# Layer 3's sums in a four-layer graph kernel: which density groups stand between the last tiles, and where the ninth tile is loaded

## The chip, the cores and the metric

The kernel runs on one core of one Trainium2 chip. The metric is the device time of one execution in microseconds. Three runs of the kernel before gave 861.08, 863.25 and 863.85 us, a median of 863.25 us. One further execution was profiled; all views below are of that one.

## The reference

Four graph layers follow one another on x (2708 nodes, 128 features) and a dense 0/1 adjacency matrix of 2708 x 2708. The change touches the fourth, called layer 3:

```python
def _L3_gnn_ref(X, A, W, a):
    XW = jnp.matmul(X, W)
    s_col = jnp.matmul(XW, a[0, :f])
    s_row = jnp.matmul(XW, a[0, f:])
    Z1 = jax.nn.leaky_relu(s_row[:, None] + s_col[None, :], negative_slope=0.01)
    den = jnp.exp(Z1)
    num = jnp.matmul(A, den)
    att = jnp.where(num != 0, den / jnp.where(num != 0, num, 1.0), 0.0)
    H = jnp.matmul(A, jnp.matmul(att, XW))
    return H
...
h = jnp.maximum(_layernorm(x, axis=-1), 0.0)
x = x + _L3_gnn_ref(h, adj, L3_gnn_W, L3_gnn_a)
```

`den[i, j]` depends only on the sum of a row score and a column score. Where that sum is positive, `den` is a product of two exponentials, and where it is negative, a product of two others. So with the nodes sorted by score, a whole chunk of nodes can be summed at once, and only the nodes near the place where the sign changes need their own values.

## The kernel before

The nodes lie in T = 22 tiles of 128, the last with 20 rows. In the general stage `rest(exact, ...)`, of which the exact variant runs with this adjacency, layer 3 goes through these steps.

1. *Ranks and chunks.* Each node's rank by score is counted, and the nodes are cut into 22 chunks (`ge`, `lt`, `wts`).
2. *Sums.* `sums(t)` (line 818) loads the 128 rows of tile t of the transposed adjacency with a DMA on the SP queue (line 826, 1354 KB by the profile's count) and multiplies them on TensorE (line 833) with two sets of chunk weights. A tile is 18 matmuls: three banks, three bf16 pieces of the weights, two halves. All 22 tiles accumulate into the same three PSUM banks, `acc` 0 to 2. Where the rows go depends on t:
   - tiles 0 to 3 (`t < NEARLY`, which is 4) go into `early_rows`: two parts of dflat, then hn, then yT;
   - three later tiles (`LATER`) go into `regained`, which are hT, row_b, hs and yT, by number: tile 8 into hs, tile 19 into hT, tile 20 into row_b;
   - all others go through the ring `steps`, tag `rows`, which has four buffers. A tile's load waits until the sums of the tile four places earlier in the ring are done.
3. *Places.* Meanwhile VectorE works out which nodes belong to which chunk, with small products on TensorE (`placed`, line 862). Its last results are the operands `c_two` and `r_hi` of the densities.
4. *Densities.* There are NS = 44 half steps, taken in eleven groups of four. `densities(s0)` (line 1080) makes a diagonal operand on VectorE (line 1084), multiplies it with ones on TensorE into a bank of the two-bank pool `ps` (line 1091), evacuates the four quarters of the bank in turn on VectorE (line 1099) and ScalarE (line 1097), and finishes with one VectorE instruction (line 1100) and one exponential on ScalarE (line 1101). The result lies in `dmat`, which is dflat.
5. *Evacuation and return.* The three banks of sums go to hn (lines 1117 and 1118), are cut into a high and a low part in yT (lines 658 and 1121), and are written to DRAM as `pre_d` by two DMAs on the SP queue and two on the ScalarE queue (line 1124). This block has raised priority.
6. *Attention loop.* For each half step the adjacency rows of 128 listed nodes are gathered into one of the four `regained` buffers (`gather_rows`, line 660), a few rows of `pre_d` are gathered over them (`carry`, line 1128), and the buffer is cast into a `rows` tile (line 1163). Both gathers are indirect DMAs issued by GpSimd (line 647). Then come products with the densities (line 1201), a logarithm (line 1206), an exponential (line 1215) and a second product (line 1145). This loop has 22 steps.

The order of instructions on each engine is fixed when the program is built. A planner takes the instruction that is earliest in the program among those that it holds ready at an estimated time; raised priority goes ahead. Instructions given to `tc.keep_in_program_order` keep their order among themselves on their engine. In the kernel before, the seven calls of `densities` up to `FIRST = 28` stand in the program ahead of `sums(4)` to `sums(21)`, the three gathers into hT, row_b and hs come after the sums, and the other four groups follow. Neither the sums nor the density products are marked, so the planner places them freely on TensorE. The products of the loop at line 1201 and 1145 are marked, and so are the row gathers and the casts.

Of the kernel before, what the change touches and what calls it, by code (L numbers as in the profile page):

```python
# [19 lines left out]
def kernel(  # L20
# [19 lines left out]
    nc = tc.nc  # L40
# [3 lines left out]
    T = -(-N // P)  # L44
# [17 lines left out]
    def rows(t):  # L62
        return min(P, N - t * P)
# [16 lines left out]
    def cols(t):  # L80
        return slice(t * P, (t + 1) * P)
# [11 lines left out]
    def bank():  # L93
        return ps.tile([P, 512], F32, tag="bank", name="bank")
# [70 lines left out]
    NS = 2 * NE  # L165
# [108 lines left out]
    with ExitStack() as stack:  # L274
# [3 lines left out]
        def load_rows(src, t):  # L278
            return fill(stream.tile([P, N], F32, tag="a", name="a"), src, t)
# [67 lines left out]
        for t in range(T):  # L347
            a = first_rows[t] if t < 3 else load_rows(adj, t)
# [119 lines left out]
    for i, at in enumerate(SUMS):  # L468
        m = (is_lo, is_hi)[i % 2]
# [16 lines left out]
    def rest(exact, stack3):  # L486
# [173 lines left out]
        def gather_rows(a, s):  # L660

            m = gather(a, adj_t[:, :], row_i[:, s : s + 1])
            tc.keep_in_program_order(m)
            return a
# [4 lines left out]
        with tc.tile_pool(name="tab", bufs=1) as tab, tc.tile_pool(name="tabs", bufs=2) as tabs:  # L669
# [17 lines left out]
            for b in range(NB):  # L687
# [26 lines left out]
                for c in range(new.start, new.stop, 3):  # L714
                    m = min(3, new.stop - c)
# [13 lines left out]
            for c in range(0, T, 3):  # L729
                m = min(3, T - c)  # L730
# [8 lines left out]
                for q in range(m):  # L739
                    t = c + q  # L740
# [77 lines left out]
            def sums(t):  # L818
                r = rows(t)
                if t < NEARLY:  # L820
                    a = early_rows[t]
                elif t in LATER:
                    a = regained[LATER[t]]
                else:
                    a = steps.tile([P, N], F32, tag="rows", name="rows")
                nc.sync.dma_start(a[:r, :], adj_t[t * P : t * P + r, :])
                if exact:
                    a = a.bitcast(BF16).rearrange("p (n h) -> p n h", h=2)[:, :, 1]
                for b in range(3):
                    for i, w in enumerate(wts):  # L830
                        for h in range(2):
                            lo, hi = BLK[b + 3 * h]
                            nc.tensor.matmul(  # L833
                                accs[b][64 * h : 64 * h + 2 * NC, : hi - lo],
                                w[:r, t, :],
                                a[:r, lo:hi],
                                start=(t == 0 and i == 0),
                                stop=(t == T - 1 and i == len(wts) - 1),
                            )

            early_rows = [dflat[:, :N], dflat[:, N : 2 * N], hn.rearrange("p t d -> p (t d)")[:, :N], yT[:, :N]]
            NEARLY = len(early_rows)

            LATER = {NEARLY + 4: 2, T - 3: 0, T - 2: 1}


            ohc = tt("ohc", [P, T, NC], ge[:, :, :NC], ge[:, :, 1:], ALU.subtract)
# [32 lines left out]
            for t in range(NEARLY):  # L880
                sums(t)
# [193 lines left out]
            r_hi = row("r_hi", NS)  # L1075
            nc.vector.tensor_scalar(r_hi, r_step, slope_hi, None, ALU.mult)

            FIRST = 28

            def densities(s0):  # L1080
                n = min(4, NS - s0)
                diag = tabs.tile([P, 4, P], F32, tag="diag", name="diag")
                z = dmat[:, s0 : s0 + n, :]
                nc.vector.tensor_tensor(
                    diag[:, :n],
                    ident[:, None, :].to_broadcast([P, n, P]),
                    c_two[:, s0 : s0 + n, None].to_broadcast([P, n, P]),
                    ALU.mult,
                )
                p = bank()  # L1090
                nc.tensor.matmul(  # L1091
                    p[:, : n * P], ones, diag[:, :n].rearrange("p s q -> p (s q)"), start=True, stop=True
                )
                for q in range(n):
                    by = r_hi[:, s0 + q : s0 + q + 1]
                    if q % 2:
                        nc.scalar.activation(z[:, q, :], p[:, cols(q)], AF.Identity, bias=by, scale=slope_hi)
                    else:
                        nc.vector.tensor_scalar(z[:, q, :], p[:, cols(q)], slope_hi, by, ALU.mult, ALU.add)
                nc.vector.scalar_tensor_tensor(z, z, flatter, z, ALU.mult, ALU.max)  # L1100
                nc.scalar.activation(z, z, AF.Exp)

            for s0 in range(0, FIRST, 4):
                densities(s0)
            for t in range(NEARLY, T):
                sums(t)
            for q in range(3):
                gather_rows(regained[q], q)
            for s0 in range(FIRST, NS, 4):
                densities(s0)  # L1110
            flat = hn.rearrange("p t d -> p (t d)")
            pre_hi = yT[:, :HALF]
# [35 lines left out]
        with tc.tile_pool(name="att", bufs=2) as attp:  # L1148
# [29 lines left out]
            for s in range(NE):  # L1178
# [19 lines left out]
                for b, (lo, hi) in enumerate(E0):  # L1198
                    num = bank()
                    for i, (d, a) in enumerate(products):  # L1200
                        m = nc.tensor.matmul(  # L1201
                            num[:, : hi - lo], d, a[:, lo:hi], start=(i == 0), stop=(i == len(products) - 1)
                        )
# [81 lines left out]
    with tc.If(some_low > 0) as general:  # L1285
        with ExitStack() as s3:
            rest(False, s3)
    with general.Else():
        with ExitStack() as s3:
            rest(True, s3)  # L1290
# [32 lines left out]
```

## Time and profile before

| what | us |
|---|---|
| median of three runs | 863.25 |
| profiled execution, whole | 860.91 |
| its span, first to last instruction | 859.1 |
| mean granted TensorE clock | 0.935 of full |
| first sums on TensorE start | 445.91 |
| last sums start (18 instructions, 2.00 us) | 520.30 |
| pre_d write leaves the queue, takes 7.80 | 527.59 |
| first product of the attention loop | 541.31 |
| first instruction of the last product's chain | 786.67 |

Times in the table are counted from the start of the span. Over the whole span TensorE's matmuls are busy for 727.6 us (85%), VectorE 583.0 us (68%), ScalarE 535.8 us (62%) and GpSimd 193.5 us (23%). These shares are means over stages with different limits, so they say little of one stage. For a change in one stage the chain of waits and the timeline there are read instead.

The SP queue, which issues the loads of the sums, looks like this between 404 and 502 us. The columns are the start, the time from the first to the last issue of the group, the engine, the line, the operation, what is written from what, and the count:

```profile
404.47 0.33 SPq L826 DMA_DIRECT2D hn<-in_adj_t_dram  x1
416.34 0.33 SPq L826 DMA_DIRECT2D hs<-in_adj_t_dram  x1
462.69 28.40 SPq L826 DMA_DIRECT2D rows<-in_adj_t_dram  x10
491.18 0.44 SPq L826 DMA_DIRECT2D hT<-in_adj_t_dram  x1
491.72 0.46 SPq L826 DMA_DIRECT2D row_b<-in_adj_t_dram  x1
501.57 0.30 SPq L826 DMA_DIRECT2D rows<-in_adj_t_dram  x1
```

The load into hn is tile 2, the one into hs is tile 8, the ten into `rows` are tiles 9 to 18, and the last four lines end with tile 19, tile 20 and the short tile 21.

### The profile page before, as it was taken

The page shows a single profiled execution, that of the slowest core. Times are in us where ns is not written, and L with a number is a line of the kernel's source. Part 1 is how long each engine was busy: PE and PEld are TensorE (multiplying, and loading weights), DVE is VectorE, ACT ScalarE, POOL GpSimd, SP SyncE. Part 2 cuts the span into 40 slices and gives each one's busy share as a digit, 9 for nine tenths or more (in the row PEclk, how much of TensorE's full clock was granted, in tenths as well). Part 3 has the DMA queues.
Part 4 walks back from the last instruction along what each step waited for, and adds up shares of the span by engine and source line. Part 5 has one row for each costly group of instructions (what it writes and reads, how often), then busy time and mean ns, then how long its engine had stood idle before and what let it go on. Part 6 is the DMA issues. An engine that isn't in the chain of part 4 may idle for free.

```text
span 859.1 us, 9007 instructions
## 1 busy us (share of the span) xinstructions
PE 727.6 (85%) x3113; PEld 436.7 (51%) x3113; DVE 583.0 (68%) x1112; ACT 535.8 (62%) x595; POOL 193.5 (23%) x161
## 2 busy tenths in 40 slices
PE   3599999995996979978659592699999999989996
PEld 2333333332775857755226331455555555555785
DVE  5499879786834263357988984566776667655854
ACT  3889999995845474446850052678777777767000
POOL 3000000012201010002000101656666666620010
PEclk9889999997897989988879997799999999999999
DMA  9034444724997989966404956677777777785993
GB/s 336 3 136 189 167 165 186 304 76 153 355 402 275 358 341 394 409 269 234 157 1 160 403 237 238 231 290 265 272 285 273 263 286 271 283 302 231 424 427 128
DMA packets 39476, 218.63 MB, mean 254 GB/s; under 512 B 5108, under 2 KB 13999, under 8 KB 25359
## 3 DMA queue, kind: packets, MB, share of 16 engines
q1 hardware_dynamic: 27704, 150.19, 45.1%
q0 software_dynamic: 8624, 65.76, 20.9%
q10 hardware_dynamic: 3090, 1.99, 0.7%
q8 instruction: 27, 0.44, 0.2%
q14 instruction: 31, 0.25, 0.1%
HBM read 214.12 MB, written 3.79 MB: 254 GB/s over the span
## 4 chain that ended last, share of the span: by engine, by line
PE 12%; DMA 10%; DVE 10%; POOL 7%; issue 7%; ACT 6%; POOLq 0%; DVEq 0%; ACTq 0%
DMA hs<-in_adj_t_dram 4%; DMA yT<-pre_d,pre_i 4%; PE acc L1145 3%; PE bank L1201 3%; PE acc L833 2%; ACT rows L1163 2%; POOL hT L647 2%; PE acc L224 2%; POOL hs L647 2%; POOL yT L647 1%; PE bank L1091 1%; POOL xw L647 1%; ACT row_a L747 1%; ACT e L1215 1%; DVE bits L744 1%
## 5 line engine op out<-in xcount | busy, mean ns | idle before, releaser
L1201 PE MATMUL bank<-rows,d_hi 128*128 128x512 f32 (+1 forms) x264 | 106.6, 408 | 37.7 <-DVE d_hi L1170 19.0
L224 PE MATMUL acc<-rows,h_hi 128*128 128x512 f32 (+1 forms) x264 | 107.1, 410 | 9.4 <-ACT rows L529 5.6
L1145 PE MATMUL acc<-e,xw 128*128 128x512 f32 (+1 forms) x264 | 104.3, 545 | 0.0
L1206 ACT ACTIVATE ln<-bank,tiny 128x512 f32<-128x512 f32 x132 | 79.6, 632 | 32.2 <-PE bank L1201 32.2
L224 PE MATMUL acc<-rows,h_lo 128*128 128x512 f32 (+1 forms) x264 | 98.6, 390 | 0.2 <-DVE h_lo L506 0.2
L1201 PE MATMUL bank<-rows,d_lo 128*128 128x512 f32 (+1 forms) x264 | 98.5, 385 | 0.0
L1201 PEld LDWEIGHTS bank<-rows,d_hi 128*128 128x128 f32 x264 | 51.2, 194 | 66.7 <-ACT ln L1206 29.1
L1209 DVE TENSOR_TENSOR e<-e,ln 128x1536 f32<-128x1536 f32 (+2 forms) x66 | 69.6, 1094 | 18.2 <-ACT ln L1206 17.9
L358 DVE SCALAR_TENSOR_TENSOR tau<-tau,e_hi,a 128x1536 f32<-128x1536 f32 (+1 forms) x44 | 70.5, 1623 | 10.2 <-DMA a<-in_adj_dram 5.5
L1145 PEld LDWEIGHTS acc<-e,xw 128*128 128x128 f32 x264 | 48.4, 190 | 52.6 <-issue 52.6
L355 ACT ACTIVATE tau<-row_a,e_neg,e_lo 128x1536 f32<-128x1536 f32 (+1 forms) x44 | 65.7, 1503 | 3.9 <-PE bank L367 3.7
L224 PEld LDWEIGHTS acc<-rows,h_hi 128*128 128x128 f32 x264 | 52.6, 200 | 24.0 <-ACT rows L529 8.5
L224 PEld LDWEIGHTS acc<-rows,h_lo 128*128 128x128 f32 x264 | 52.7, 200 | 12.2 <-issue 2.2
L367 PE MATMUL bank<-tau,ones_at 128*32 128x512 f32 (+1 forms) x264 | 51.8, 566 | 8.3 <-DVE tau L358 8.3
L224 PE MATMUL acc<-yT,hs 128*128 128x512 f32 x132 | 56.7, 567 | 0.0
L1215 ACT ACTIVATE e<-e 128x2708 f32<-128x2708 f32 x22 | 54.2, 2462 | 3.2 <-DVE e L1209 3.2
L224 PE MATMUL acc<-row_b,hs 128*128 128x512 f32 x132 | 55.3, 557 | 0.0
L1201 PEld LDWEIGHTS bank<-rows,d_lo 128*128 128x128 f32 x264 | 51.5, 195 | 7.1
L224 PE MATMUL acc<-rows,y_hi 128*128 128x512 f32 x132 | 49.2, 379 | 4.8 <-DVE rows L1278 2.9
L224 PE MATMUL acc<-rows,y_lo 128*128 128x512 f32 x132 | 47.7, 376 | 0.0
L529 ACT CAST rows<-dflat 128x1536 fp32r<-128x1536 f32 (+1 forms) x26 | 34.2, 1330 | 20.7 <-DMA dflat<-in_adj_dram 11.6
L173 POOL TENSOR_TENSOR rstd<-isq,neg_half 128x4 f32<-128x4 f32 (+1 forms) x24 | 23.5, 982 | 99.8 <-DVE isq L172 85.0
(411 smaller groups left out, 1394.8 us busy)
## 6 DMA issues: line engine op xcount, KB each, us to landing
a<-in_adj_dram SPq DMA_DIRECT2D x21, 1354.0 KB
rows<-in_adj_t_dram SPq DMA_DIRECT2D x17, 1354.0 KB
dflat<-in_adj_t_dram SPq DMA_DIRECT2D x9, 768.0 KB
rows<-in_adj_t_dram SPq DMA_DIRECT2D x9, 768.0 KB
dflat<-in_adj_dram SPq DMA_DIRECT2D x9, 768.0 KB
rows<-in_adj_dram SPq DMA_DIRECT2D x9, 768.0 KB
dflat<-in_adj_t_dram SPq DMA_DIRECT2D x5, 1354.0 KB
hs<-in_adj_t_dram SPq DMA_DIRECT2D x5, 1354.0 KB
```

The lines of the kernel that those rows point to most:

```text
L173: nc.gpsimd.tensor_tensor(dst, s[:, :n], neg_half[:, :n], ALU.pow)
L224: nc.tensor.matmul(accs[b][:, : hi - lo], w, moving[:, lo - at : hi - at], start=start and i == 0, stop=stop and i == len(parts) - 1,)
L355: nc.scalar.activation(tau[:, :w], row_a[:, h0:h1], AF.Relu, bias=e_neg[:, t : t + 1], scale=e_lo[:, t : t + 1])
L358: nc.vector.scalar_tensor_tensor(tau[:, :w], tau[:, :w], e_hi[:, t : t + 1], a[:, h0:h1], ALU.add, ALU.mult)
L367: nc.tensor.matmul(den[g : g + 32, : hi - lo], ones_at[:, b // GR, :], tau[:, lo - h0 : hi - h0], start=(t == 0 and b < GR), stop=(t == T ...
L529: m = nc.vector.tensor_copy(r, a) if i % 2 and i > 4 else nc.scalar.copy(r, a)
L647: return nc.gpsimd.indirect_dma_start(out=out, out_offset=None, in_=src, in_offset=bass.IndirectOffsetOnAxis(ap=idx, axis=0),)
L1145: m = nc.tensor.matmul(accs[b][:, : hi - lo], xw, e[:, lo:hi], start=(s == 0), stop=(s == NE - 1))
L1201: m = nc.tensor.matmul(num[:, : hi - lo], d, a[:, lo:hi], start=(i == 0), stop=(i == len(products) - 1))
L1206: nc.scalar.activation(ln[:, lo:hi], num[:, : hi - lo], AF.Ln, bias=tiny)
L1209: tc.keep_in_program_order(nc.vector.tensor_sub(e[:, beg:hi], e[:, beg:hi], ln[:, beg:hi]))
L1215: tc.keep_in_program_order(nc.scalar.activation(e, e, AF.Exp))
```

## The change

It has four parts.

1. Tile 8 is loaded into `early_rows[2]`, the hn buffer that tile 2 had. Tile 9 takes hs. The ring `rows` then holds 14 tiles of the sums in place of 15.
2. The matmuls of the sums from tile 8 on are marked to keep their program order.
3. The matmul of each density group is marked in the same way.
4. `FIRST` is 3 and counts groups. In the program no group stands ahead of the sums; one group follows each of `sums(17)`, `sums(18)` and `sums(19)`. The other eight groups follow the three gathers.

```diff
                 if t < NEARLY:
                     a = early_rows[t]
+                elif t == NEARLY + 4:
+                    a = early_rows[2]
                 elif t in LATER:
                     a = regained[LATER[t]]
...
-                            nc.tensor.matmul(
+                            m = nc.tensor.matmul(
                                 accs[b][64 * h : 64 * h + 2 * NC, : hi - lo],
...
+                            if t >= NEARLY + 4:
+                                tc.keep_in_program_order(m)
...
-            LATER = {NEARLY + 4: 2, T - 3: 0, T - 2: 1}
+            LATER = {NEARLY + 5: 2, T - 3: 0, T - 2: 1}
...
-            FIRST = 28
+            FIRST = 3
...
                 p = bank()
-                nc.tensor.matmul(
+                m = nc.tensor.matmul(
                     p[:, : n * P], ones, diag[:, :n].rearrange("p s q -> p (s q)"), start=True, stop=True
                 )
+                tc.keep_in_program_order(m)
...
-            for s0 in range(0, FIRST, 4):
-                densities(s0)
             for t in range(NEARLY, T):
                 sums(t)
+                if T - 2 - FIRST <= t < T - 2:
+                    densities(4 * (t - T + 2 + FIRST))
             for q in range(3):
                 gather_rows(regained[q], q)
-            for s0 in range(FIRST, NS, 4):
+            for s0 in range(4 * FIRST, NS, 4):
                 densities(s0)
```

## Prediction

> **What bounds the kernel now.** I read the page's slices first, then the chain of waits around layer 3's sums, then each engine's timeline there, then windows. The slices show where to look: TensorE's busy row falls to 1 in one slice of the last third, at about 525 to 540 us.
>
> ```profile
> PE   3599999995996979978659592699999999989996
> DMA  9034444724997989966404956677777777785993
> ```
>
> The chain, from the last sums to the first step of the attention loop (columns: start, us, what):
>
> ```profile
> 508.82 1.05 PE bank L1091 x2
> 509.88 2.13 PE acc L833 x18
> 512.01 1.92 PE bank L1091 x4
> 513.92 1.93 PE acc L833 x18
> 515.85 1.07 PE bank L1091 x2
> ...
> 526.87 0.62 DVE yT L1121
> ...
> 527.59 7.80 DMA pre_d<-yT
> ...
> 536.39 3.04 DMA hT<-pre_d,pre_i
> ...
> 539.45 1.59 DVE rows L1163
> ```
>
> L833 is the sums, L1091 the density products. They alternate on one chain, so each density group ahead of the last sum delays everything below: evacuating the sums, writing them to pre_d, gathering them back, the loop. TensorE's timeline gives the ends (the bracket is idle time before):
>
> ```profile
> 485.03 5.53 PE L833 MATMUL acc<-rows,wts 128*44 128x450 bf16 x39
> 494.59 3.68 PE L1091 MATMUL bank<-diag,ones 128*128 128x512 f32 x4 [4.03 <-DVE diag L1084]
> ...
> 520.30 2.00 PE L833 MATMUL acc<-rows,wts 20*44 20x452 bf16 x18
> 541.31 0.77 PE L1201 MATMUL bank<-rows,d_hi 128*128 128x512 f32 x1 [19.01 <-DVE d_hi L1170]
> ```
>
> The sums end at E = 522.3 (520.30 + 2.00). TensorE has stood 4.03 us for the first density operand, and then 19.01 us for the gathered sums. Windows tell whether the sums could have been earlier (columns: window, length, then busy us of PE, PEld, DVE, ACT and POOL, clock, DMA share, GB/s):
>
> ```profile
> 484.60:499.40 14.80, 10.77 (x59) 4.30 (x57) 12.66 (x31) 1.59 (x4) 4.07 (x4) 0.77 0.98 391
> 499.40:506.20 6.80, 6.80 (x38) 2.41 (x37) 5.69 (x12) 4.22 (x9) 0.00 (x0) 1.00 0.99 401
> 506.20:518.60 12.40, 11.98 (x66) 4.40 (x64) 10.65 (x23) 7.60 (x17) 0.94 (x1) 1.00 0.09 18
> ```
>
> Until 506.2 the adjacency rows stream at 390 to 400 GB/s; then DMA is idle (share 0.09) for 12 us with TensorE full. So up to 506 the rows are the bound, and from there TensorE, by the density products. Adding up the bytes of the sync queue's packets, in tiles of 1.387 MB, gives the landings: tile 9 at 468.0, 12 at 478.0, 15 at 488.3, 16 at 492.2, 17 at 495.9, 18 at 499.4, 19 at 502.7, 20 (with the short tile 21) at 506.1: 3.47 us each on average.
>
> **What the Trainium skill says.** (1) "PSUM — Partial Sum Buffer", Engine vs sequencer instructions: matmuls start and complete in program order, and the ScalarE and VectorE queues are strict FIFO. The trace agrees: by the landings tile 15 was there at 488.3, but its sums stood behind the density product that waited to 494.59. (2) The same page, PSUM bank collisions: two engines must not touch one bank and quadrant together, ScalarE beside VectorE included. So the four quarters of a density bank go one after another; the trace shows 0.41 us on VectorE and 0.46 us on ScalarE in turn. (3) "DMA: Bandwidth & Descriptors", Issuing engines are not separate DMA queues: all share 16 engines. The pre_d write (4 x 232.7 KB) took 7.80 us with three row gathers of 1.387 MB in flight. (4) "TensorE: Matmul & The Clock Gate", Part 1: idle TensorE drops to half clock. The four L1091 after the 4.03 us idle took 3.68 us, where later pairs take 1.05.
>
> **The change part by part.**
>
> *Eight of eleven density groups leave the stretch of the sums.* A group costs TensorE one pair, 1.05 us. Removed from TensorE before E: 8 x 1.05 = 8.4 us, and the 4.03 us wait with its slow first products (3.68 - 2.10 = 1.6 us), since tiles 15 to 17 now come ahead of the first density product. Without the rows' bound that is 14.0 us, E = 508.3.
>
> *The three groups that stay.* The fixed order is tile 17, group 0, tile 18, group 1, tile 19, group 2, tile 20, tile 21. A tile's 18 sums take 1.93 us, a group 1.05: 2.98 together, less than the 3.47 us between landings, so the rows hide them. Group 0's operand is ready at 494.55 as before (VectorE's chain to L1084 isn't touched). Sums of tile 17 end about 495.4, so the new fixed wait holds nobody; behind it stand tile 18 and all later sums, which have not landed.
>
> *The ninth tile.* Tile 8 goes to hn, free when tile 2's sums end (453.9), in place of hs, which it had from 416.34; hs takes tile 9, and the ring of four holds 14 tiles in place of 15. Before, the sync queue stood from 416.74 to 462.69 for the first ring slot, with DMA idle. Now tile 9 can load at 416 and tile 8 at 454 in that idle time; tile 8 is needed at 467.7 and takes some 2 + 3.3 us, so it is there at about 459.3. This costs nothing (if SP has it behind the ring's load instead, it lands near 468, some 0.5 us late). After 462.7 one tile less is to load: tile 20 lands one tile earlier, about 502.8. Against that: a ring slot opens only when its sums are done, and TensorE stands at L862 to 483.42 for VectorE. If L862 keeps its place inside tile 12's sums, tile 16's load starts 2.5 us late. The planner may place L862 a tile later, which costs nothing. I take half, so 504.1; ends 502.8 and 505.3.
>
> *The new end.* Sums started 1.3 us after the landing (tile 11: 474.76 to 476.06). E = 504.1 + 1.3 + 2 x 1.93 = 509.3, gain 13.0; 508.0 to 511.3 if the landing is 502.8 to 506.1.
>
> *After E.* The three gathers on the POOL queue follow the sums of tiles 19 and 20 and the free hs: about E - 5.4, E - 1.5, E - 0.2, where before they went at E - 5.65, E - 1.15 and E + 0.46. So pre_d meets the same traffic, and its 7.80 us stays. Evacuation (522.21 to 527.5) has raised priority and stays E + 5.2. The gathered sums are cast (L1163) at E + 17.15.
>
> *Where the eight groups go.* Their products need 8.4 us of an idle TensorE. Their elementwise half is dearer: without TensorE in the way the period was 1.8 us a group:
>
> ```profile
> 517.30 0.75 DVE L1100 SCALAR_TENSOR_TENSOR dflat<-dflat,flatter 128x512 f32<-128x512 f32 x1
> ...
> 519.10 0.75 DVE L1100 SCALAR_TENSOR_TENSOR dflat<-dflat,flatter 128x512 f32<-128x512 f32 x1 [0.20 <-ACT dflat L1097]
> ...
> 520.89 0.75 DVE L1100 SCALAR_TENSOR_TENSOR dflat<-dflat,flatter 128x512 f32<-128x512 f32 x1 [0.72 <-ACT dflat L1097]
> ```
>
> 8 x 1.8 = 14.4 us from E + 5.2 is E + 19.6, about E + 19 with what fits into the evacuation's gaps. The cover ends at E + 17.15; past it the casts for the loop queue behind on VectorE. I charge 2.0 us; ends 0 (the casts go ahead, and only TensorE's first products are late) and 7 (2.36 us a group, the period while TensorE was shared: 5.2 + 18.9 - 17.15). TensorE may enter the loop warmer: its first 9 products took 0.63 us, later ones 0.39, at most 9 x 0.24 = 2.2 us; taken as nothing, because the chain at the loop's start runs through gathers and casts.
>
> *Sum.* 13.0 - 2.0 = 11.0 us. The loop (541 to 787) and the last product start from this point and shift whole. On the profiled execution (860.91 us, span 859.1) that is 849.9. It lies 2.3 us under the median of 863.25, and the same 11.0 us against the median gives 852.2: **852**.
>
> **Rivals.** *A, the cover is full:* casts are not delayed, and the rows come at the early end: 522.3 - 508.0 = 14.3 us, 849. For it: later groups are first needed several loop steps on. Against: a FIFO VectorE with 14.4 us of work in a 12 us gap.
>
> *B, a small gain:* ring slots open late (landing 506.1, E = 511.3, gain 11.0), and the groups run at 2.1 us, halfway between the two periods, so 16.8 + 5.2 - 17.15 = 4.9 us late: gain 6.1, 857. For it: 9.3 us of waiting for sums on the sync queue before the last row load. Against: that load was 0.2 MB and late for nobody.
>
> *C, slower:* the evacuation's copies get queued behind the density groups on VectorE and ScalarE; one in-order queue then holds back pre_d. Price: 1.8 to 2.36 us for each group ahead, against 13.0 of gain; it decides from 5.5 to 7.2 groups on. All eight at 2.36 us: 18.9 - 13.0 = 5.9 us slower, 869; at 1.8, 1.4 slower. For it: the queues are fixed when the kernel is built, on estimated times. Against: the copies carry raised priority, and the groups' products stand behind the last sums on TensorE, so they can't be ready sooner.
>
> *D, it cancels:* C's mechanism with about seven groups, 863; or the fixed order changes little, since the planner had already put the sums where they now are. Against the latter: seven groups before E in the chain above and in TensorE's timeline.
>
> **How the numbers follow.** Forecast 0.58 (848 to 856), A 0.12, B 0.15, C 0.11, D 0.04. 846.5 to 859 takes in the forecast, A and B and leaves out C, D and a little: about 0.17. A measurement here tells 0.3%, 2.6 us, from no change. Faster 0.58 + 0.12 + 0.15 = 0.85; same 0.04; slower 0.11.
>
> **What would show it.** Right: TensorE's timeline has tiles 15 to 17 ahead of the first L1091, just three pairs before the last sums, these ending near 509, and eight pairs in the former 19 us idle; DMA waits return before the sums of tiles 18 to 20; the first L1201 comes near 530. Wrong: sums still ending past 515; evacuation copies starting later than 1 us after E; the cast L1163 more than 4 us behind its gather; or a loop longer than 245 us, which gives the gain back. A tile 8 waited for near 468 would show the buffer swap as a cost.

## The result, and the profile after

The changed kernel takes 852.05 us (median of four runs, 850.04 to 853.49) against 863.15 us before (four runs, 861.08 to 863.85): a ratio of 0.9874 with a 95% interval from 0.9847 to 0.9900. A second set, six runs against sixteen, gave 853.77 and 863.58 us, ratio 0.9880 (0.9850 to 0.9911). The forecast was 852.

The slices of the page show the hole filled: the digit 1 in TensorE's row has gone.

```profile
PE   3599999995996979978649785798999989989997
```

TensorE's timeline of the changed kernel, from the first sums (L835 is the sums, L1095 the density products, L1206 the loop's first product, L1150 its second; the bracket is idle time before):

```profile
444.04 0.95 PE L835 MATMUL acc<-dflat,wts 128*44 128x452 bf16 x4 [5.04 <-DVE wts L813]
...
483.19 7.30 PE L835 MATMUL acc<-rows,wts 128*44 128x450 bf16 x57
493.00 3.45 PE L835 MATMUL acc<-rows,wts 128*44 128x452 bf16 x18 [2.51 <-DMA rows<-in_adj_t_dram]
496.39 1.12 PE L1095 MATMUL bank<-diag,ones 128*128 128x512 f32 x2
...
499.37 1.12 PE L1095 MATMUL bank<-diag,ones 128*128 128x512 f32 x2
...
502.35 1.13 PE L1095 MATMUL bank<-diag,ones 128*128 128x512 f32 x2
...
505.53 2.00 PE L835 MATMUL acc<-rows,wts 20*44 20x452 bf16 x18
507.46 1.98 PE L1095 MATMUL bank<-diag,ones 128*128 128x512 f32 x4
513.57 4.25 PE L1095 MATMUL bank<-diag,ones 128*128 128x512 f32 x4 [4.12 <-DVE diag L1088]
...
533.44 0.76 PE L1206 MATMUL bank<-rows,d_hi 128*128 128x512 f32 x1 [4.70 <-DVE d_hi L1175]
...
550.88 4.75 PE L1150 MATMUL acc<-e,xw 128*128 128x512 f32 x12
```

Three groups stand between the last sums, TensorE waits for a row load (2.51 us) instead of a density operand, and the sums end at 507.5. The chain of waits now has the load of tile 20 in it, where it had sums and density products in turn:

```profile
488.25 15.31 DMA row_b<-in_adj_t_dram
...
503.60 3.12 PE acc L835 x27
```

The chain gives this stretch to the load, but only just: from 493.00 to the end of the sums TensorE has no wait longer than 0.12 us, because the sums of tile 17 took 3.45 us behind their wait (granted clock 0.53) where a tile takes 2.00 elsewhere. In a second profile of the changed kernel they took 2.00, and TensorE waited 0.82, 0.18 and 0.79 us for tiles 18, 19 and 20; there the rows hide the three groups.

The windows agree (window, length, busy us of PE, PEld, DVE, ACT and POOL, clock, DMA share, GB/s). The rows run out in the window from 499.40 (share 0.50), and the window that had DMA idle at share 0.09 now has the gathers in it:

```profile
499.40:506.20 6.80, 6.67 (x50) 2.94 (x50) 4.95 (x9) 3.11 (x7) 0.94 (x1) 1.00 0.50 162
506.20:518.60 12.40, 7.48 (x23) 2.32 (x19) 10.21 (x22) 5.75 (x13) 1.88 (x2) 0.78 0.92 368
```

What came before the first sums differed by 1.9 us between the two first profiles, with the same work in it, so distances are counted from the first sums. With a second profile of each kernel, in us:

| distance | before | before again | changed | changed again |
|---|---|---|---|---|
| first sums to end of last sums (E) | 76.4 | 77.6 | 63.5 | 63.2 |
| E to the loop's first product | 19.0 | 19.0 | 25.9 | 25.8 |
| first sums to the loop's first second product | 114.0 | 116.1 | 106.8 | 106.1 |
| the loop, first product to last second product | 245.1 | 246.5 | 245.3 | 243.7 |
| span | 859.1 | 860.0 | 851.7 | 850.7 |

The means give 13.6 us gained at E, 6.8 at the loop's first product, 8.6 at its first second product and 8.4 in the span. The timed runs say 10 to 11. The distances inside the loop differ by 1 to 2 us between two profiles of one kernel, so small differences there say little.

### The profile page after: what moved, and what is told of

It is laid out like the page before. It is cut to its first block, busy times and chain, and to the rows that moved or that the text cites. A ratio compares the mean times of both kernels' runs of the same rounds, so it can differ in the third digit from the quotient of the medians.

```text
span 851.7 us, 9005 instructions
## 1 busy us (share of the span) xinstructions
PE 729.7 (86%) x3113; PEld 440.8 (52%) x3113; DVE 583.7 (69%) x1112; ACT 536.1 (63%) x595; POOL 189.2 (22%) x161
## 4 chain that ended last, share of the span: by engine, by line
PE 14%; DMA 12%; DVE 9%; issue 6%; POOL 6%; ACT 5%; SPq 0%; DVEq 0%; POOLq 0%; ACTq 0%
PE acc L1150 4%; PE bank L1206 4%; DMA hs<-in_adj_t_dram 4%; DMA row_b<-pre_d,pre_i 3%; PE acc L835 2%; DMA row_b<-in_adj_t_dram 2%; ACT rows L1168 2%; POOL hT L647 2%; POOL hs L647 1%; DMA yT<-pre_d,pre_i 1%; PE acc L224 1%; POOL row_b L647 1%; ACT row_a L747 1%; DVE rows L1283 1%; DVE bits L744 1%
## 5 line engine op out<-in xcount | busy, mean ns | idle before, releaser
L1206 PE MATMUL bank<-rows,d_hi 128*128 128x512 f32 (+1 forms) x264 | 106.5, 408 | 24.4 <-ACT ln L1211 12.7
L224 PE MATMUL acc<-rows,h_hi 128*128 128x512 f32 (+1 forms) x264 | 106.5, 408 | 10.3 <-ACT rows L529 6.0
L1150 PE MATMUL acc<-e,xw 128*128 128x512 f32 (+1 forms) x264 | 104.3, 545 | 0.0
L1206 PE MATMUL bank<-rows,d_lo 128*128 128x512 f32 (+1 forms) x264 | 98.7, 385 | 0.0
L1214 DVE TENSOR_TENSOR e<-e,ln 128x1536 f32<-128x1536 f32 (+2 forms) x66 | 70.0, 1097 | 15.9 <-ACT ln L1211 15.6
L1206 PEld LDWEIGHTS bank<-rows,d_hi 128*128 128x128 f32 x264 | 51.6, 195 | 53.1 <-ACT ln L1211 31.7
L1150 PEld LDWEIGHTS acc<-e,xw 128*128 128x128 f32 x264 | 48.4, 190 | 52.6 <-issue 52.6
L1206 PEld LDWEIGHTS bank<-rows,d_lo 128*128 128x128 f32 x264 | 51.6, 195 | 7.0
L1189 DVE TENSOR_SCALAR xw<-xw,c_exp 128x128 f32<-128x128 f32 x22 | 6.4, 290 | 58.2 <-DMA xw<-xw_d,xw_i 58.2
```

Source lines behind the costliest of these rows:

```text
L224: nc.tensor.matmul(accs[b][:, : hi - lo], w, moving[:, lo - at : hi - at], start=start and i == 0, stop=stop and i == len(parts) - 1,)
L1150: m = nc.tensor.matmul(accs[b][:, : hi - lo], xw, e[:, lo:hi], start=(s == 0), stop=(s == NE - 1))
L1206: m = nc.tensor.matmul(num[:, : hi - lo], d, a[:, lo:hi], start=(i == 0), stop=(i == len(products) - 1))
L1214: tc.keep_in_program_order(nc.vector.tensor_sub(e[:, beg:hi], e[:, beg:hi], ln[:, beg:hi]))
```

## The experiments

Edits are to the changed kernel where nothing else is said. A time given for "first product" alone is counted from the first sums, and E is the end of the last sums, given as a distance from the first ones. The letters T and R stand for the theories and rivals of the expectation quoted above each result.

**The changed kernel again.**

> The changed kernel once more, for a second profile and more times. In its first profile the last sums ended 12.9 us earlier than before, counted from the first sums, but the loop's first product came only 6.0 us earlier: the density groups after the sums cost 6.9 us, not the 2.0 us of the prediction. Theory T (half-clock density products and one VectorE queue make the tail 6.9 us): the same distances again, 63.5 us from the first to the end of the last sums and 89.4 us to the loop's first product, each within 0.5 us, and a time of 852 us within 2. Rival R (the first profile was an odd execution; the tail costs 2.0 us as predicted): the loop's first product near 84.5 us after the first sums.

Measured: E 63.2, first product 89.0; 853.77 us. The long tail comes again, so it isn't one odd execution, and R falls. What it consists of is asked further down.

**The swap alone**, on the kernel before:

```diff
+                elif t == NEARLY + 4:
+                    a = early_rows[2]
...
-            LATER = {NEARLY + 4: 2, T - 3: 0, T - 2: 1}
+            LATER = {NEARLY + 5: 2, T - 3: 0, T - 2: 1}
```

> Only the ninth tile's buffer changes; the groups stay where they were and nothing is marked. If TensorE with seven groups between the sums is the bound (T): rows land one tile earlier, but the sums still end 74 to 76.4 us after the first sums, and the time is 861 to 863 us. Rival (the row loads were the bound and the swap carries the gain): 855 us or less.

Measured: 856.75 us, ratio 0.9921 (0.9897 to 0.9946). E is 75.7, as T had it, with eleven pairs still ahead of it; but the time fell by more than T allowed, and by less than the rival asked. The rest came after E: the loop's first product follows it by 16.4 us in place of 19.0. GpSimd's timeline shows the first row gather:

```profile
514.27 1.40 POOL L647 DMA_INDIRECT hT<-in_adj_t_dram,row_i  x1 [21.61 <-ACT dflat L1099]
```

That is 7.6 us ahead of E (521.8), where before it was 5.65; the third gather went 2.5 us ahead of E, where before it went 0.46 behind it. TensorE's timeline shows why:

```profile
515.31 2.00 PE L835 MATMUL acc<-row_b,wts 128*44 128x452 bf16 x18
517.24 1.13 PE L1093 MATMUL bank<-diag,ones 128*128 128x512 f32 x2
518.78 1.12 PE L1093 MATMUL bank<-diag,ones 128*128 128x512 f32 x2 [0.42 <-ACT dflat L1099]
519.84 2.00 PE L835 MATMUL acc<-rows,wts 20*44 20x452 bf16 x18
```

The planner now has the last two groups behind the sums of tile 20. Before, they stood ahead of these sums (pairs at 515.78 and 517.32, the sums at 518.38). The second gather needs row_b, which tile 20's sums free, and the third is issued behind it, so both could start sooner. The gathers were further on when pre_d was written, and the chain has:

```profile
526.55 5.89 DMA pre_d<-yT
```

5.89 us in place of 7.80. So this gain comes from the order that the planner made of the same instructions, and not from the landing at E. The profile has some 3 to 4 us of the 6.8 in these stages. The profiled execution itself, at 858.14 us, was only 2.8 and 3.7 us below the two of the kernel before, so it can't show the rest, which stays unexplained.

**The move alone**, with the two swap lines taken back:

> The groups move and are marked as in the change, but tile 8 stays in hs, so one tile more is loaded through the ring. By the prediction's sum the last tile lands one tile later, so the sums end about 3.4 us later than in the changed kernel, some 67 us after the first sums, and the time is about 855 us. Rival (the load of tile 8 in the idle time is worth nothing): 852 us.

Measured: E 66.7, first product 92.5, 855.97 us (0.9873 to 0.9932 of before), close to T on both. One ring tile more is worth 3.4 us at E. By the medians the two parts alone give 6.8 and 7.6 us and together 9.8; with intervals of some 2.5 us to each side, how much they overlap is not settled. At E they don't: 1.3 and 10.3 us there, and 13.6 together.

**The tail left out.** The eight groups after the sums are dropped, and a memset gives their densities the value one:

```diff
+            nc.gpsimd.memset(dmat[:, 4 * FIRST :, :], 1.0)
...
-            for s0 in range(4 * FIRST, NS, 4):
-                densities(s0)
```

> The changed kernel without the eight density groups after the sums; GpSimd sets their densities to one instead, so this part of the computation is left out. T: the loop's first product comes 19 us after the end of the sums, 82.5 us after the first sums, 6.9 us less than in the changed kernel, and the time is about 845 us. R (tail costs 2.0 us): 850 us.

Measured: 848.87 us, 4.9 below the changed kernel measured beside it (853.77). E was 64.8 here, 1.4 us later than with the tail (why isn't shown), and the first product came 19.4 us after it (19.0 before). So at that product the tail costs 6.5 us, and T is right there. But the loop's first second product came 105.5 us after the first sums, hardly sooner than with the tail (106.1 and 106.8). The ScalarE cast that leads to it shows one reason:

```profile
539.84 2.45 ACT L1167 CAST rows<-yT 128x2708 fp32r<-128x2708 f32 x1 [0.57 <-DMA yT<-pre_d,pre_i]
```

It waits for the gathers into yT, 94.5 us after the first sums; in the changed kernel it starts at 97.0 with the tail. So the gathers take up part of what the first product gains. The other reason is TensorE's clock. Of the 40 products of 512 columns ahead of the first second product, 27 took 0.58 us or more here (granted clock 0.50 from 529.5 to 536.3 and from 543.6 to 550.1), and only 15 and 14 in the two profiles with the tail; the others took about 0.40. Some 1.6 us ahead of the first second product, this kernel and then the changed one:

```profile
549.29 0.63 PE L1205 MATMUL bank<-rows,d_lo 128*128 128x512 f32 x1
```

```profile
549.20 0.40 PE L1206 MATMUL bank<-rows,d_lo 128*128 128x512 f32 x1
```

Set at the same E, the tail costs 2.4 us at the first second product (43.1 us after E against 40.7), but twelve or thirteen more slow products, at some 0.2 us each, can account for up to an estimated 2.5 us of what was left of the gain, and these belong to the clock and not to the tail. Compared with the kernel before, where that distance was 37.6 and 38.5 us, the changed kernel's is 5.0 longer. The timed runs agree with the larger cost: 4.9 us less at an E that came 1.4 later. Neither the 845 of T nor the 850 of R was met; the first product came 1.7 us later than T had it, most of it at E.

**The kernel before again.**

> The kernel before once more, for a second profile. Its first profiled execution took 860.9 us, at the low end of its timed runs of 859 to 867 us. Theory T (the fixed instruction order gives the same distances): the sums end 76.4 us after the first sums and the loop's first product comes 95.4 us after them, each within 1 us, and the rest of the gap to the median lies outside these stages. Rival (the stretch of the sums itself varies from run to run in the kernel before, with the TensorE clock, so the first profile understates the gain): one of the two distances is 2 us or more longer.

Measured: 861.78 us in 14 runs (859.24 to 865.05), E 77.6, first product 96.6. E is 1.2 us longer than in the first profile. The timeline shows where:

```profile
493.20 3.78 PE L1091 MATMUL bank<-diag,ones 128*128 128x512 f32 x4 [4.05 <-DVE diag L1084]
496.91 2.45 PE L833 MATMUL acc<-rows,wts 128*44 128x452 bf16 x11
```

Eleven sums took 2.45 us where they took 1.37 in the first profile: after the wait for the operand the half clock lasted longer (granted clock 0.50 over these sums, and 1.00 in the first profile). At 1.2 us this is outside the 1 us of T and goes the rival's way, but is under the rival's 2.

**Without the marks.**

```diff
-                            if t >= NEARLY + 4:
-                                tc.keep_in_program_order(m)
...
-                tc.keep_in_program_order(m)
```

> The changed kernel without the two marks, so the planner may place the density products among the sums again. If the marks only confirm an order that the planner would choose (theory T): 852 to 854 us as with them. Rival (the planner moves groups of the tail ahead of the last sums, since their operands are ready in its estimate): more than three and a half pairs before the end of the sums, the sums ending 2 us or more later, and 855 us or more.

Measured: 855.71 us (0.9889 to 0.9950 of before), E 74.4. The rival was right; the end of TensorE's timeline has the planner's order:

```profile
515.45 1.98 PE L1093 MATMUL bank<-diag,ones 128*128 128x512 f32 x4
517.36 1.99 PE L835 MATMUL acc<-rows,wts 20*44 20x452 bf16 x18
```

All eleven pairs are again ahead of the last sums. The place in the program by itself moves no group behind them; this kernel is in effect the swap alone (ratio 0.9920, and 0.9921 there). Both marks were taken away at once, so which of them is needed isn't shown.

**TensorE kept busy in the tail**, with products of ones on a spare bank:

```diff
+            spare_bank = acc_bank(5)
             for s0 in range(4 * FIRST, NS, 4):
                 densities(s0)
+                for _ in range(4 if s0 == 4 * FIRST + 4 else 1):
+                    m = nc.tensor.matmul(
+                        spare_bank, ones, ident[:, None, :].to_broadcast([P, 4, P]), start=True, stop=True
+                    )
+                    tc.keep_in_program_order(m)
```

> The changed kernel with idle products on a spare bank between the density products of the tail, one after each group and four in the 4 us gap, so that TensorE does not stand idle there. Theory T1 (the tail is long because the density products run at half clock, 2.1 in place of 1.05 us a pair, and VectorE waits for them): the loop's first product comes 2 to 3.5 us sooner after the end of the sums than the 25.9 us of the changed kernel, and the time falls by as much. Theory T2 (the tail is the sum of VectorE's own work and its hand-overs with ScalarE): the distance changes by less than 1 us and the time stays at 852 to 854 us.

Measured: first product 24.5 us after E, 1.4 less; 851.82 us. Windows over the same stretch, first of the changed kernel, then of this one:

```profile
507.50:533.40 25.90, 13.93 (x17) 3.73 (x16) 20.70 (x42) 13.79 (x27) 7.88 (x7) 0.61 0.64 247
```

```profile
507.50:533.40 25.90, 19.36 (x53) 7.29 (x49) 20.95 (x43) 14.79 (x29) 7.84 (x7) 0.97 0.65 243
```

The clock goes from 0.61 to 0.97 and a pair from 2.1 to 1.1 us, but VectorE's work (20.7 and 21.0 us of 25.9) is what it was. Half clock is 1.4 us of the tail, between T1 and T2; the timed runs don't separate this kernel from the changed one.

**The groups moved into the loop**, one after each of its steps 1 to 8. The products are marked as in the changed kernel; the groups' instructions on VectorE and ScalarE are not, unlike the loop's own. Their operands c_two, r_hi and diag are also kept in a pool that lasts through the loop (not shown):

```diff
-            for s0 in range(4 * FIRST, NS, 4):
-                densities(s0)
...
                 done[s] = (xw, e)
+                if 1 <= s and 4 * (s + FIRST - 1) < NS:
+                    densities(4 * (s + FIRST - 1))
```

> The changed kernel with its eight late groups moved on, one after each of the loop's steps 1 to 8, where each is still ahead of its first use. The loop's first product should then come about 19.4 us after the end of the sums, as where the groups were left out, 6.5 us sooner than in the changed kernel. If the loop's early steps wait for gathers and have room on TensorE and VectorE: about 847 us. If the loop is full, so that the groups cost there what they cost before it (1.05 us of TensorE and 1.9 us of VectorE each): 852 us or more.

Measured: 905.63 us (1.0464 to 1.0533). The first product did come 19.5 us after E, but the loop took 304.5 us. Per group that is (304.5 - 245) / 8 = 7.4 us, more than a group's own work. The waits of the window from 525 to 640 (engine, line, waited for: us in total, times, longest):

```profile
DVE dflat L1103 <- PE bank L1094: 25.7, 3, 9.5
```

VectorE stood in its queue for density products that come late in a step, up to 9.5 us at once, and the loop's instructions stood behind. Steps 1 to 8 took 16 to 20 us each, most later ones 10 to 11 as elsewhere. A version with these instructions placed by hand wasn't tried.

**Four and five groups between the sums.** `FIRST = 4` and `FIRST = 5`:

> The changed kernel with FIRST = 4: one group more between the sums, after tile 16, where TensorE stood 2.5 us for tile 17 anyway, and seven after them. If each group of the tail delays the loop (theory T, 25.9 - 19.4 = 6.5 us over eight groups, or 2 to 2.6 us for each at the margin): the sums end within 1 us of the changed kernel's 63.3 us after the first sums, the loop's first product comes about 2 us sooner after that, 87.5 us after the first sums, and the time is about 850 to 851 us. If the last group is covered as the prediction had it: no change from 852 to 853 us.

> FIRST = 5: the first group follows tile 15, and TensorE waits there some 3 us for its operand with tile 16 landed behind it. T: the sums end about 2 us later than with three groups, 65.5 us after the first sums, the tail is 4 to 5 us shorter, and the loop's first product comes 86.5 to 87.5 us after the first sums; 850 to 851 us. If the fixed wait costs more than the two groups save: 853 us or more.

Four: E 63.0, first product 86.1, 850.21 us, ratio 0.9851 (0.9821 to 0.9880). The fourth group fits into the 2.5 us in which TensorE waited for tile 17 (it now waits 2.36 us for this group's operand), and the tail is 2.8 us shorter, as T had it. It is the lowest ratio of the kernels that compute everything, though its interval overlaps that of the changed kernel. Five: E 68.4, first product 91.3, 855.51 us. The fixed place after tile 15 stops TensorE until the operand is there:

```profile
494.63 2.08 PE L1095 MATMUL bank<-diag,ones 128*128 128x512 f32 x2 [4.14 <-DVE diag L1088]
496.63 3.58 PE L835 MATMUL acc<-rows,wts 128*44 128x452 bf16 x18
```

It loses 4.14 us there, and a tile's sums then take 3.58 us in place of 2.00 (granted clock 0.50). T was wrong here and its rival right: the fixed wait costs more than the two groups save. Marks make a fixed order, and in it the operand's time decides.

**One engine for each late group.**

```diff
-                    if q % 2:
+                    if (s0 // 4 if s0 >= 4 * FIRST else q) % 2:
```

> The changed kernel with the four quarters of a late group evacuated by one engine, VectorE for even groups and ScalarE for odd ones, so the hand-overs inside a bank go while VectorE's total work stays (1.92 us a group). If the hand-overs make the tail's period 2.6 us (T2a): the loop's first product comes 1.5 to 3 us sooner than the 25.9 us after the sums, about 850.5 us. If VectorE's total work and its order with the loop's casts set it (T2b): less than 1 us, 852 to 853 us.

Measured: first product 23.9 us after E, 2.0 less; 850.38 us, ratio 0.9870 (0.9843 to 0.9898). T2a holds in the profile: giving each bank to one engine is worth 2.0 us there, inside the 1.5 to 3 expected for the hand-overs. The timed runs don't separate it from the changed kernel.

**All three together**, four between, one engine per group, busy TensorE:

> The changed kernel with four groups between the sums, one engine per late group, and idle products that keep TensorE at full clock in the tail. Alone these brought the loop's first product to 86.1, 87.7 and 87.8 us after the first sums, from 89.2. The bound without any tail is 82.5 (E 63.2 and 19.4 after it). If they act on different parts of the tail: about 84.5 us and 848 us. If they remove the same wait: 86 us and 850 us.

Measured: the first product at 83.6, better than either expectation, and 852.43 us (0.9876 to 0.9922), no gain at all. The loop took 248.6 us. Its first second product came at 104.9 us, where four groups alone gave 104.6. As with the tail left out, 27 of the 40 products ahead of it took 0.58 us or more. This is no fixed floor: with the groups in the loop the first second product came at 103.4, with 18 such products. Why the later steps took longer here isn't shown.

## Why the prediction was right, and where it was off

The total was 11.0 us and the timed runs gave 9.8 and 11.1. The mechanism came as forecast up to E; the cost of the tail was too small. Step by step:

- *Rows.* Tile 20 was to land at 504.1 on the clock of the first profile (502.8 to 505.3). By the packets' bytes it landed at 501.2, which is 503.0 on that clock. The products of L862 stand one tile further on than before, inside tile 13's sums: the case that costs nothing; the prediction had taken the middle of the two. Right within the ends given.
- *E.* Gain 13.0 predicted; 12.9 between the first profiles, 13.6 between the means. Right in size, and the move alone puts the ring tile at 3.4 us, the value used. But two errors cancel: the landing came 1.1 us early, and from this count of the landing to E it took 6.3 us in place of 5.2 (1.3 + 2 x 1.93). The chain has the load of tile 20 end at 503.56, 2.4 us after that count, where the prediction allowed 1.3.
- *Evacuation and return.* The carry gather was issued at 521.25, 13.7 us after E; before it was 14.1. Right. In the second profile it was issued 15.6 us after E, and the first product still came at 25.8, so the return wasn't what that product waited for.
- *The tail.* "I charge 2.0 us" for casts behind the groups is the term that was mis-sized. The cast L1168 did start at 527.45, 19.9 us after E, 2.8 us past its due time. But VectorE's order put more behind it:

```profile
527.45 1.56 DVE L1168 CAST rows<-hT 128x2708 fp32r<-128x2708 f32 x1
528.93 0.74 DVE L1105 SCALAR_TENSOR_TENSOR dflat<-dflat,flatter 128x512 f32<-128x512 f32 x1
...
531.47 0.41 DVE L1104 TENSOR_SCALAR dflat<-bank,slope_hi,r_hi 128x128 f32<-128x128 f32 x1 [1.48 <-ACT dflat L1102]
532.40 0.75 DVE L1105 SCALAR_TENSOR_TENSOR dflat<-dflat,flatter 128x512 f32<-128x512 f32 x1 [0.53 <-ACT dflat L1102]
533.07 0.22 DVE L1175 CAST d_hi<-dflat 128x128 fp32r<-128x128 f32 x1
```

The loop's operand d_hi stands behind the last two groups, and these wait for ScalarE, which is in its own cast (528.12 to 530.56). So the first product was 6.9 us later after E, the upper end that the prediction named, not its value. The period of 1.8 us a group was read where TensorE was at full clock; at a mean clock of 0.61, and with the cast among them, it was 2.6 (513.94 to 532.40 over seven groups). The runs give 1.4 us of the tail to the clock and 2.0 to the hand-overs, each taken away alone; the rest is argued from the order above.

- *The loop shifts whole.* From first product to last second product its length hardly changed (245.8 us before and 244.5 after, on average). Of the 6.9 us, 1.8 came back by the first second product, which leaves 5.0 there and 5.2 in the span. That is the size of the tail in these profiles, against the 2.0 charged. The warmer TensorE at the loop's start, taken as nothing, was small: 8 and 7 of the first step's products took 0.58 us or more, and 9 and 12 before.

So 13.6 at E less 5.2 is the 8.4 us of the four profiles, and not 11.0. The timed medians, 9.8 and 11.1, are no contradiction: the interval of the larger set reaches from 0.9% to 1.5%, or 7.7 to 13.0 us, and both profiled executions of the kernel before, 860.91 and 861.79, lie below the medians of the two sets, 863.15 and 863.58. But the number was hit in part by luck. On the execution from which it was worked out, the sum forecast 849.9 us; the two profiled executions of the changed kernel took 853.49 and 852.45. The 852 comes from setting the same sum against the slower median.

The timed runs of the kernel before scatter from 859 to 867 us. The half clock after its 4 us wait, 1.2 us different between two profiles, may be a part of that; this was not shown.

Of the rivals, A's full cover didn't come, and B's late ring slots didn't either; but B's other half, a tail 4.9 us late, is close to what the profiles show. C was excluded as argued: the evacuation started at once after E, with two density quarters between its last instructions. D's remark of "seven groups" was a slip: the timeline before has eleven pairs ahead of E, as the sum of eight removed and three kept assumes. D's other half, that the order changes little, is what the kernel without marks does.

## What to carry to other kernels

When loads bound a stretch, give the gaps between them as much other work as fits, and no more: three or four groups here, while a fifth, put ahead of its own operand, cost 5 us at the end of the sums. Work moved behind the critical step isn't free when the next stage's operands go through the same in-order queue; look at what is queued ahead of the first operand of that stage, not only at its first cast. Check in the timeline as well that a move in the program moved the instructions: without the order marks all eleven products went back.

## What was not expected of the hardware

The four products after a wait of about 4 us ran at half clock (granted clock 0.50 to 0.53; 3.68, 3.78 and 4.25 us for two pairs, where two pairs take 1.98 at full clock), and how long that lasted differed from run to run of one kernel: about 3.5 us in one profile of the kernel before and 6.2 in the other, so that the eleven sums after the products took 1.37 us and 2.45. After a wait of 2.5 us it could come or not: a tile's sums took 3.45 us behind a wait of 2.51 in the changed kernel and 2.00 behind one of 2.52 with the tail left out.

The write of pre_d took from 5.89 to 9.50 us in the seven profiles whose chain shows it. It ended 12.6 to 13.8 us after the third row gather was issued in all seven, whether it began 4.3 us after that gather or 7.6. That suggests that the gathers ahead of the write set when the sums are back, and not the write's own start; no run moved the gathers alone.
